# Half-row products for the multipliers, a run of zero products, and finer ranks in a sequence mixer with grouped linear layers

## The chip, the core and the metric

The kernel runs on one NeuronCore of a Trainium2 chip. The metric is the device time of one execution in microseconds (us), lower is better. TensorE (PE) multiplies, VectorE (DVE) and ScalarE (ACT) do arithmetic per element, GpSimd (POOL) does some too, and SyncE (SP) issues nearly all DMA transfers. Everything is float32.

## The reference

```python
x = x + attn(layernorm(x))          # x: 4 x 2048 x 256
x = x + ffn(layernorm(x))
# attn: u, v = split(silu(xn @ uv_w));  out = (u * tno(v)) @ o_w
#   tno: y = irfft(rfft(a, 2n) * rfft(v, 2n))[:n], a long convolution along the sequence;
#   a comes from a small network of the lag (rpe: 4 layers of width 32, layer norm and silu,
#   then @ rpe_out_w), times 0.99**|lag|
# ffn: 8 groups of 1024 tokens; h = (x @ W1[g].T + b1[g]) @ W2[g].T + b2[g]
```

The two linear layers of the ffn have nothing between them, so the kernel multiplies the two matrices of a group into one of 256 x 256. The convolution is done in eight residues r of the sequence: split into rings, a product with cosines and sines (forward), a product with the spectrum of a (the multipliers), a product back, and a recombination.

## The kernel before, in words

`rpe_network` computes the small network for all lags, in two halves of 512 columns: per layer a product `ph`, squares and a copy by ACT (`sq`, `d`), sums `pvar` by PE, an inverse root in eleven small DVE operations (`nve` to `ne`), transposes `pr` and the activation `z`. It is one long dependent chain. `rpe_transform` turns z into the multipliers: DVE forms `rr`, `rq` and `rqd`; per residue r two products make `hp`, DVE multiplies it by phases (`tr`), and products with the weight `wz` make `pa`, which ACT and DVE copy to `am_d` (r = 0) and `am_c` (r = 1 to 7). In `wz`, 128 x 512, the four blocks of 32 rows hold the same weight in one of two halves of the columns, and zeros elsewhere; each `pa` is one product over 128 rows and 512 columns, one for each half k of the frequencies.

`stage_a(b, q)` normalizes a quarter of batch b, transposes it (`pt_a`), and multiplies to `v` (`pv`). `gate` makes u (`pu`, `gt`). `prepare(b, h)` splits v of one half of the channels into rings (DVE). `stage_b(b, h)` gives `forward(r)` (products `pf`, DVE products `y` and `far` with `am`), `backward(r)` (products `acc`), `after(r)` and `end` (DVE: `id`, `iw`, `x0`, `x1`, `x2`, `p`, `tk`; POOL multiplies `gt` by `tk`). `stage_d(b, q)` multiplies `gt` by `ow` (`po`), adds x, normalizes, transposes (`pt_d`), multiplies by the combined matrix `wt` (`pff`), and stores. `stage_w(g)` makes `wt`: four pairs of loads of 256 KB each, a bias by ACT, four products `pw` for each pair. Two pairs fit at once (`WB = 2`); the tables `mats` of the forward and backward products have three buffers each.

No engine's order is that of the program text. Every operation is recorded with a rank, `issue_order` simulates the engines with estimated costs and buffers, and whenever an engine could start several operations it takes the earliest, and of those with the same time the one of lowest rank. The result is a fixed order for each engine, executed in that order; DMA loads stand in SP's order in the same way. Ranks come from `PLACE` by way of `place`: one number for a stage, a quarter or a residue, moved by 20 for each batch. All operations of, say, `forward(r)` (its load, its products, its DVE work) share one.

All recorded operations carry one line number in the profile, L1019, so they are told apart by the names of their tiles.

Of the kernel before, what the change touches and what calls it, by code (L numbers as in the profile page):

```python
# [38 lines left out]
P = 128  # L39
# [10 lines left out]
LAG = 2  # L50
# [56 lines left out]
class Operation:  # L107
# [8 lines left out]
    def cost(self, method):  # L116

        n, psum = columns(self.outs[0]), [a.space == PSUM for a in self.ins]
        if self.dma:
            return (400 if self.engine == "SP" else 460), n * P * 4 / 250  # L120
        if self.engine == "PE":
            return (2 if method == "matmul" else 1) * max(n * 0.84, 110), 165
# [18 lines left out]
class Pool:  # L141
# [5 lines left out]
    def tile(self, shape, dtype, name, **kw):  # L147
# [5 lines left out]

PLACE = {
    "a first": (-99.0, -98.0, -97.0, -96.0),
    "a": (1.74, -2.67, 2.51, 4.46),
    "b": (
        (6.26, 12.16, 4.1, 8.11, 8.37, 13.79, 12.58, 14.11),
        (10.46, 20.27, 15.97, 19.01, 18.94, 18.98, 20.74, 20.97),
    ),  # L160
    "d": (
        (25.35, 27.7),
        (26.25, 28.74),
        (30.44, 33.54),
        (29.38, 31.46),
    ),
    "d last": (
        (42.27, 25.3),
        (65.21, 140.66),
        (46.22, 27.3),  # L170
        (61.26, 28.3),
    ),
    "e": (
        (14.31, 18.21, 18.05, 16.77, 63.85, 71.2, 77.59, 18.72, 12.6, 21.84, 13.2),
        (20.2, 20.5, 20.8, 19.37, 21.4, 39.89, 22.0, 22.54, 22.6, 28.52, 26.75),
    ),
    "e last": (20.2, 100.83, 20.8, 21.1, 21.4, 111.26, 22.0, 22.3, 22.6, 22.9, 23.2),
    "f": (
        (2.08, 2.91, 1.13, 2.05, 4.0, 3.57, 6.5, 6.26),
        (4.04, 18.16, 13.91, 14.02, 14.8, 14.19, 17.79, 18.04),  # L180
    ),
    "g first": (
        (-95.0, 1.77, -95.0, -40.12),
        (-95.0, -95.0, -95.0, -95.0),
    ),
    "g": (
        (6.27, 12.71, 15.72, 5.68),
        (13.81, 10.75, 16.06, 24.4),
    ),
    "p first": (21.76, -4.4, -4.1, -3.8, -3.5, -23.28, -84.19, -2.6, -2.3, -2.0, -1.7, -1.4, -1.1, -0.8, -0.5, 5.66),  # L190
    "p": (
        (55.79, 1.74, 22.08, 23.91, 1.63, 19.64, 38.78, 19.76, 4.06, 16.19, 4.2, 33.43, 39.59, 10.38, 4.51, 33.61),
        (14.03, 5.6, 11.32, 67.54, 11.67, 6.8, 14.31, 16.92, 15.07, 18.9, 70.61, 20.64, 18.53, 20.4, 45.22, 86.73),
    ),
    "rpe": -100.0,
    "rpet": -10.0,
    "w": (-52.41, -95.4, 43.06, 31.0, 55.36, 77.26, 90.91, 188.4),
# [3 lines left out]
def place(stage, *i):  # L201
    if stage in ("rpe", "rpet"):
        return (PLACE[stage],)
    if stage == "w":
        return (PLACE["w"][i[0]] + 0.1 * i[1],) if i[0] < WT else (PLACE["w"][i[0]] + i[1],)
    b, *i = i
    if b == 0 and (stage in ("a", "g") or (stage == "p" and i[0] == 0)):
        stage, i = stage + " first", i[1:] if stage == "p" else i
    elif b == B - 1 and (stage == "d" or (stage == "e" and i[0] == 1)):
        stage, i = stage + " last", i[1:] if stage == "e" else i  # L210
    at = PLACE[stage]
    for n in i:
        at = at[min(n, len(at) - 1)]
    return (20 * b + at,)


# [3 lines left out]
def issue_order(ops, tags):  # L220
# [43 lines left out]
    while len(order) < len(ops):  # L264
# [5 lines left out]
        free[o.engine] = at + o.busy  # L270
        end = at + o.busy + o.tail
# [24 lines left out]
def kernel(  # L296
# [49 lines left out]
    am_c = [const.tile([P, 2, 2, 2, P], F32, name=f"am{r}") for r in range(NR)]  # L346

# [147 lines left out]
    def stage_a(b, q):  # L495
        xnt = xnts[b, q] = tok.tile([P, 2, 4 * P], F32, tag="xnt", bufs=4, name=f"xnt_{b}_{q}")
        xt = early.pop((b, q), None) or load_x(b, q, "xa")
        name = f"a{b}_{q}"
        transposed(normalized(xt, *statistics(xt, name, on_scalar=b > 0), name), xnt, name)
# [11 lines left out]
        r, j0 = divmod(2 * q, 4)  # L511
        for h in range(2):
            lo, hi = (v[:, :, i, h * P : (h + 1) * P] for i in range(2))
            c = cts[b, h]
            G.tensor_tensor(c[:, r, j0 : j0 + 2, 0, :], hi, lo, ALU.add)
            a_, b_ = (lo, hi) if r else (hi, lo)
            G.tensor_tensor(c[:, 1 - r, j0 : j0 + 2, 1, :], a_, b_, ALU.subtract)
# [22 lines left out]
    def rpe_network():  # L540
# [7 lines left out]
        early.update({(0, q): load_x(0, q, "xa") for q in range(2)})  # L548
        decay = t4("decay", "f4")[:, :NT]
        S.dma_start(decay, decays)  # L550

# [17 lines left out]
        for i in range(L + 1):  # L569
            sqs, ds = [], []  # L570
# [25 lines left out]

        z = t4("z", "i4").rearrange("p (j f) -> p j f", f=F)
# [10 lines left out]
    def load_phases():  # L608
        phs = [io.tile([P, 4, D], F32, tag="xd", name=f"ph_{i}") for i in range(2)]
        for i in range(2):  # L610
            for k in range(2):
                S.dma_start(
                    phs[i][k * 64 : (k + 1) * 64], phases[k, 4 * i : 4 * i + 4].partition_broadcast(64)
                )
        return phs

    def rpe_transform(z, phs):
        wz = t4("wz", "i4")[:, : 4 * P].rearrange("p (r c) -> p r c", r=2)
        V.memset(wz, 0.0)
        for s_ in range(4):  # L620
            A.dma_start(wz[s_ * F : (s_ + 1) * F, s_ % 2, :], out_w)
# [41 lines left out]
        for pos, (r, eng) in enumerate(((0, V), (1, V), (1, None), (0, V))):  # L663
            for xx in range(2):
                dst = rq[:, 1:, xx, pos, :]
                if eng is None:
                    A.mul(dst, rv[:, :, r, xx, :], -1.0)
                else:
                    eng.tensor_copy(dst, rv[:, :, r, xx, :])
# [6 lines left out]
        V.tensor_copy(rqd[:, :, 1, 1, :], rdv[:, :, 1, :])  # L676
        A.mul(rqd[:, :, 1, 2, :], rdv[:, :, 1, :], -1.0)


        for r in range(NR + 1):  # L680
            m = ring_mats(r, 0, f"rpe_{r}")
            ph = ps_f.tile([P, 2 * P], F32, tag="pf", name=f"hp{r}")
# [14 lines left out]
            V.tensor_tensor(tr, ph, phs[r // 4][:, r % 4, :], ALU.mult)  # L697
            for k in range(2):
                pa = ps_mm.tile([P, 2, D], F32, tag="mm", name=f"pa{r}_{k}")
                T.matmul(  # L700
                    pa.rearrange("p r c -> p (r c)"),
                    tr[:, k * P : (k + 1) * P],
                    wz.rearrange("p r c -> p (r c)"),
                    start=True,
                    stop=True,
                )
                src = pa.rearrange("p r (h c) -> p h r c", h=2)
                if r == 0:
                    A.copy(am_d[:, :, 0:3:2, k, :], src)
                    V.tensor_copy(am_d[:, :, 1, k, :], src[:, :, 0, :])  # L710
                elif k:
                    A.copy(am_c[r - 1][:, :, :, k, :], src)
                else:
                    V.tensor_copy(am_c[r - 1][:, :, :, k, :], src)
# [7 lines left out]
    def stage_w(g):  # L722
        na, oc = INTER // P, 2
        yield
# [4 lines left out]
        S.dma_start(row, b2[g : g + 1, :].partition_broadcast(P))  # L729
        d = small.tile([P, na], F32, tag="d", bufs=2, name=f"dw_{g}")  # L730
# [4 lines left out]
        for o in range(0, na, oc):  # L735
            w1s = io.tile([P, oc, D], F32, tag="w1", bufs=WB, name=f"w1_{g}_{o}")
            S.dma_start(w1s, w1[g].rearrange("(p a) h -> p a h", a=na)[:, o : o + oc, :])
            w2s = io.tile([P, oc, D], F32, tag="w2", bufs=WB, name=f"w2_{g}_{o}")
            S.dma_start(w2s, w2t[g].rearrange("(p a) h -> p a h", a=na)[:, o : o + oc, :])
            for a in range(oc):  # L740
# [11 lines left out]
            yield  # L752
# [38 lines left out]
    def stage_b(b, h):  # L791
# [10 lines left out]
        def forward(r):  # L802
            m = ring_mats(r, 0, f"{nm}_{r}")
            pf = ps_f.tile([P, 2, 2, P], F32, tag="pf", name=f"pf_{nm}_{r}")
            for k in range(2):
                cols = slice(k * P, (k + 1) * P)
                for xx in range(2):
                    if r == 0:
                        T.matmul(pf[:, k, xx, :], m[:, xx, cols], rs[r][:, k, xx, :], start=True, stop=True)
                    else:  # L810
                        T.matmul(pf[:, k], m[:, xx, cols], rs[r][:, :, xx, :], start=(xx == 0), stop=(xx == 1))
            y = ys[r] = t2(f"y_{nm}_{r}", "y").rearrange("p (k r c) -> p k r c", k=2, r=2)
# [13 lines left out]
        def backward(r):  # L826
            m, y = ring_mats(r, 1, f"{nm}_{r}"), ys.pop(r)
            acc = accs[r] = ps_i.tile([P, 2, 2, P], F32, tag="acc", name=f"acc_{nm}_{r}")
# [14 lines left out]
        def after(r):  # L843
            acc = accs.pop(r)
# [82 lines left out]
    def stage_d(b, q):  # L927
        wt, last = wts[2 * b + q // 2], b == B - 1
        xt = load_x(b, q, "xa" if last and q >= 2 else "xd")
        for j in range(2):  # L930
# [12 lines left out]
        name = f"d{b}_{q}"  # L943
        xns = normalized(xt, *statistics(xt, name, on_scalar=not last), name)
        yield
        transposed(xns, xn2, name, shift=True)
        for j in range(2):
# [8 lines left out]
            if last:  # L956
                S.dma_start(out[b, q][:, r, :], xt[:, r, :])
        if not last:
            S.dma_start(out[b, q], xt)
        yield  # L960
# [3 lines left out]
    def pieces(stage, *rank):  # L964

        n = 0
        while True:
            ops.at(*place(*rank, n))
# [5 lines left out]
    def at(*rank):  # L974
        ops.at(*place(*rank))
# [3 lines left out]
    for q in range(NQ):  # L979
        at("a", 0, q)  # L980
        stage_a(0, q)
    for g in range(WT):
        list(pieces(stage_w(g), "w", g))
# [3 lines left out]
    list(pieces(prepare(0, 0), "p", 0, 0))  # L987
    for b in range(B):
        for h in range(2):
            for q in range(NQ):  # L990
                at("g", b, h, q)
                gate(b, h, [q])
        for h in range(2):
            forward, backward, after, end = stage_b(b, h)
            for r in range(NR + 1 + LAG):
                if r <= NR:
                    at("f", b, h, r)
# [124 lines left out]
```

## Time and profile before

| what | value |
|---|---|
| median of three executions | 589.51 us (589.31 to 590.65) |
| profiled execution, its own time | 589.18 us |
| its span, first to last instruction | 587.3 us |
| PE busy | 563.2 us, 96% |
| DVE busy | 504.4 us, 86% |
| ACT busy | 312.8 us, 53% |
| POOL busy | 149.7 us, 25% |
| DMA, mean | 139 GB/s |

The page gives one profiled execution. A product of float32 stands in it as two records, each with a record of a weight load. A record's duration holds its way through the array too, so the rate of PE is read from the starts of a row of records and not from their durations. Where a busy share is 100%, PE may still run below its rate.

### The profile page before, as it was taken

How to read it: one execution, taken by the hardware profiler on the slowest of the kernel's cores; microseconds unless marked ns; L12 is line 12 of the kernel's file. 1: busy time of each engine (PE TensorE's matmuls, PEld its weight loads, DVE VectorE, ACT ScalarE, POOL GpSimd, SP SyncE). 2: the span in 40 equal slices, each digit the busy share in tenths (PEclk: the TensorE clock that was granted, in tenths of full speed). 3: DMA queues.
4: the chain of work that ended last, by engine and by line, in shares of the span. 5: the costliest groups of instructions: out<-in, count | busy, mean ns of one | idle time of the engine just before them, and what ended most of it. 6: DMA issues, size and time to landing. Idle time of an engine off the chain costs nothing.

```text
span 587.3 us, 8243 instructions
## 1 busy us (share of the span) xinstructions
PE 563.2 (96%) x2620; PEld 457.3 (78%) x2620; DVE 504.4 (86%) x1118; ACT 312.8 (53%) x822; POOL 149.7 (25%) x184
## 2 busy tenths in 40 slices
PE   6899999999997999999999999999999999998797
PEld 3788565887885888787878888778888888787686
DVE  3575984999998799999986999998979999999862
ACT  2779862164322754996545728886348365112162
POOL 0154210011362211123475200106271100020420
PEclk9999999999999999999999999999999999999999
DMA  8731374555454445363541453455443543424202
GB/s 266 204 113 61 89 230 154 157 165 161 142 146 136 109 145 171 108 228 114 157 119 46 153 179 127 145 179 145 125 108 90 193 158 143 149 67 138 78 37 108
DMA packets 39987, 81.36 MB, mean 139 GB/s; under 512 B 5636, under 2 KB 7172, under 8 KB 39944
## 3 DMA queue, kind: packets, MB, share of 16 engines
q1 hardware_dynamic: 39208, 79.91, 44.2%
q10 hardware_dynamic: 736, 0.92, 0.5%
q8 instruction: 21, 0.34, 0.2%
q14 instruction: 22, 0.18, 0.1%
HBM read 72.43 MB, written 8.39 MB: 138 GB/s over the span
## 4 chain that ended last, share of the span: by engine, by line
PE 88%; DMA 7%; ACT 2%; DVE 1%; issue 1%; SPq 0%; ACTq 0%; DVEq 0%
PE acc L1019 18%; PE pf L1019 18%; PE pff L1019 9%; PE pv L1019 9%; PE po L1019 9%; PE pw L1019 7%; PE pu L1019 7%; DMA w<-in_L_ffn_W_dram 6%; PE pt_a L1019 2%; PE pa L1019 2%; PE pt_d L1019 2%; PE ph L1019 2%; PE pvar L1019 1%; PE hp L1019 1%; PE pr L1019 1%; DMA lag_t<-in_lag_rows_dram 1%
## 5 line engine op out<-in xcount | busy, mean ns | idle before, releaser
L1019 PE MATMUL acc<-mats,y 128*128 128x256 f32 (+1 forms) x512 | 114.7, 367 | 0.0
L1019 PEld LDWEIGHTS acc<-mats,y 128*128 128x128 f32 x512 | 91.7, 190 | 14.0 <-issue 2.1
L1019 PE MATMUL pw<-w,w 128*128 128x256 f32 x256 | 65.9, 388 | 11.5 <-DMA w<-in_L_ffn_W_dram 9.7
L1019 POOL TENSOR_TENSOR gt<-gt,tk 128x512 f32<-128x512 f32 x32 | 44.8, 1411 | 122.8 <-DVE tk L1019 122.8
L1019 POOL TENSOR_TENSOR c<-v 128x256 f32<-128x256 f32 x64 | 55.5, 894 | 56.2 <-ACT v L1019 45.8
L1019 PEld LDWEIGHTS pw<-w,w 128*128 128x128 f32 x256 | 46.8, 194 | 21.9 <-ACT w L1019 13.6
L1019 PE MATMUL pv<-uvw,xnt 128*128 128x256 f32 x256 | 60.7, 382 | 0.0
L1019 PE MATMUL po<-ow,gt 128*128 128x256 f32 x256 | 60.2, 379 | 0.0
L1019 ACT ACTIVATE w<-w,dw 128x256 f32<-128x256 f32 x64 | 29.6, 502 | 56.9 <-DMA w<-in_L_ffn_W_dram 56.9
L1019 PE MATMUL pu<-xnt,uvw 128*128 128x512 f32 x128 | 59.8, 592 | 0.0
L1019 PE MATMUL pf<-ra,mats 128*128 128x256 f32 x256 | 58.9, 380 | 0.0
L1019 PE MATMUL pff<-wt,xn 128*128 128x256 f32 x256 | 58.0, 380 | 0.3 <-ACT xn L1019 0.3
L1019 PEld LDWEIGHTS pv<-uvw,xnt 128*128 128x128 f32 x256 | 47.4, 190 | 8.3 <-ACT xnt L1019 1.2
L1019 PEld LDWEIGHTS pf<-ra,mats 128*128 128x128 f32 x256 | 48.2, 190 | 7.0 <-issue 0.5
L1019 PEld LDWEIGHTS pff<-wt,xn 128*128 128x128 f32 x256 | 48.1, 190 | 6.8 <-ACT xn L1019 0.6
L1019 PEld LDWEIGHTS po<-ow,gt 128*128 128x128 f32 x256 | 47.8, 190 | 7.0 <-issue 1.0
L1019 DVE TENSOR_TENSOR y<-y,far 128x256 f32<-128x256 f32 x128 | 51.8, 445 | 0.2
L1019 POOL TENSOR_TENSOR rs_a<-ve_a,mhalf 128x4 f32<-128x4 f32 x16 | 19.8, 1236 | 113.3 <-ACT ve_a L1019 105.2
L1019 POOL TENSOR_TENSOR rs_d<-ve_d,mhalf 128x4 f32<-128x4 f32 x16 | 16.6, 1037 | 115.4 <-ACT ve_d L1019 99.2
L1019 DVE TENSOR_TENSOR y<-pf,am 128x512 f32<-128x512 f32 x56 | 38.3, 684 | 6.5 <-PE pf L1019 5.0
L1019 ACT COPY e<-acc 128x512 f32<-128x512 f32 x24 | 14.0, 584 | 50.5 <-PE acc L1019 43.6
L1019 DVE TENSOR_TENSOR far<-pf,am 128x512 f32<-128x512 f32 x56 | 38.1, 681 | 0.2
(151 smaller groups left out, 1022.0 us busy)
## 6 DMA issues: line engine op xcount, KB each, us to landing
mats<-in_mats_dram SPq DMA_DIRECT2D x128, 256.0 KB, 2.7
w<-in_L_ffn_W_dram SPq DMA_DIRECT2D x64, 256.0 KB, 4.2
xa<-in_x_dram SPq DMA_DIRECT2D x18, 512.0 KB, 3.7
xd<-in_x_dram SPq DMA_DIRECT2D x14, 512.0 KB, 3.5
out_dram<-xd SPq DMA_DIRECT2D x12, 512.0 KB, 2.7
mats_rpe<-in_mats_dram SPq DMA_DIRECT2D x8, 256.0 KB, 4.1
row<-in_L_ffn_b_dram SPq DMA_DIRECT2D x8, 128.0 KB, 4.8
ph<-in_phases_dram SPq DMA_DIRECT2D x4, 256.0 KB, 5.5
```

The lines of the kernel that those rows point to most:

```text
L1019: ops[k].call(*ops[k].args, **ops[k].kw)
```

## The change

1. `wz` becomes 128 x 256: all four blocks of 32 rows hold the weight, with no zeros. The order of the four blocks in `rq` and `rqd` changes, so that rows 0 to 63 of `tr` give the real parts and rows 64 to 127 the imaginary parts. Each residue has four products of 64 rows and 256 columns in place of two of 128 rows and 512 columns. They name a position in the array: rows from 0 or rows from 64. The copies from `pa` are divided by real and imaginary part. The phases are loaded in eight transfers of 128 KB, not in four of 256 KB.
2. Eight products of zeros, 128 x 256, are ranked ahead of everything else.
3. Load, statistics, transposes, products and DVE work of a stage each get a rank of their own, with own values for the first and the last batch, and all are new. In the planner, the cost of a product is halved where it names a position and doubled ahead of 7.5 us, and transfers are taken as 270 bytes per ns of their true number of partitions.

```diff
-            return (400 if self.engine == "SP" else 460), n * P * 4 / 250
+            return (400 if self.engine == "SP" else 460), n * self.outs[0].shape[0] * 4 / 270
...
-            return (2 if method == "matmul" else 1) * max(n * 0.84, 110), 165
+            tiles = 2 if "tile_position" in self.kw else 1
+            return (2 if method == "matmul" else 1) * max(n * 0.84, 110) / tiles, 165
...
-    "rpe": -100.0,
-    "rpet": -10.0,
-    "w": (-52.41, -95.4, 43.06, 31.0, 55.36, 77.26, 90.91, 188.4),
+    "rpe": -91,
+    "rpe.0": -182,
...
+    "w.1": -95.3, "w.1.l.1": -84, "w.1.l.2": -95.1, "w.1.l.3": -58, "w.1.m.1": -95.2, "w.1.m.2": -77, "w.1.m.3": -86,
...
+    "warm": -199,
...
+COLD, WARM_UP = 7500, 8
...
-        free[o.engine] = at + o.busy
-        end = at + o.busy + o.tail
+        busy = o.busy * (2 if o.engine == "PE" and at < COLD else 1)
+        free[o.engine] = at + busy
+        end = at + busy + o.tail
...
-            for k in range(2):
+            for k in range(4):
                 S.dma_start(
-                    phs[i][k * 64 : (k + 1) * 64], phases[k, 4 * i : 4 * i + 4].partition_broadcast(64)
+                    phs[i][k * F : (k + 1) * F], phases[k % 2, 4 * i : 4 * i + 4].partition_broadcast(F)
...
-        wz = t4("wz", "i4")[:, : 4 * P].rearrange("p (r c) -> p r c", r=2)
-        V.memset(wz, 0.0)
+        wz = t4("wz", "i4")[:, :D]
         for s_ in range(4):
-            A.dma_start(wz[s_ * F : (s_ + 1) * F, s_ % 2, :], out_w)
+            A.dma_start(wz[s_ * F : (s_ + 1) * F], out_w)
...
+            pas = [ps_mm.tile([P, 2, D], F32, tag="mm", name=f"pa{r}_{c}") for c in range(2)]
             for k in range(2):
-                pa = ps_mm.tile([P, 2, D], F32, tag="mm", name=f"pa{r}_{k}")
-                T.matmul(
-                    pa.rearrange("p r c -> p (r c)"),
-                    tr[:, k * P : (k + 1) * P],
-                    wz.rearrange("p r c -> p (r c)"),
-                    start=True,
-                    stop=True,
-                )
-                src = pa.rearrange("p r (h c) -> p h r c", h=2)
...
+                for c, pa in enumerate(pas):
+                    rows = slice(c * 2 * F, (c + 1) * 2 * F)
+                    T.matmul(
+                        pa[:, k, :], tr[rows, k * P : (k + 1) * P], wz[rows], start=True, stop=True, tile_position=(c * 2 * F, 0)
+                    )
+            re, im = (pa.rearrange("p k (h c) -> p h k c", h=2) for pa in pas)
+            if r == 0:
+                A.copy(am_d[:, :, 0], re)
+                V.tensor_copy(am_d[:, :, 1], re)
+                A.copy(am_d[:, :, 2], im)
+            else:
+                A.copy(am_c[r - 1][:, :, 1], im)
+                V.tensor_copy(am_c[r - 1][:, :, 0], re)
...
+    at("warm")
+    zeros = const.tile([P, 2 * P], F32, name="zeros")
+    V.memset(zeros, 0.0)
+    warm = ps_w.tile([P, 2, D], F32, tag="w", name="warm")
+    for _ in range(WARM_UP):
+        T.matmul(warm[:, 0, :], zeros[:, :P], zeros, start=True, stop=True)
```

The order of instructions that follows differs on every engine. Some of it: on SP, the loads of `par` and `lag_t`, first and second before, stand fifth and seventh, behind the bias, the row and the first pair of weights of group 1, and the second quarter of x that is loaded is the fourth (`xa_0_3`). On PE, three `pw` of group 1 stand between the zeros and the first `ph`. The first `hp` is that of residue 2, then 4 and 1, with 0 and 5 among the first `pf`. In the last batch the four weight groups of `pw_6` and `pw_7` each stand one place earlier.

## The prediction

> **What bounds the kernel now.** I read the page first: the shares, the slices, the chain.
>
> ```profile
> span 587.3 us, 8243 instructions
> ...
> PE 563.2 (96%) x2620; PEld 457.3 (78%) x2620; DVE 504.4 (86%) x1118; ACT 312.8 (53%) x822; POOL 149.7 (25%) x184
> ...
> PEclk9999999999999999999999999999999999999999
> ...
> PE 88%; DMA 7%; ACT 2%; DVE 1%; issue 1%; SPq 0%; ACTq 0%; DVEq 0%
> ```
>
> PE bounds it, with DVE close behind. Only two things can shorten it: less PE work, or less time in which PE stands or runs slowly. So I counted PE's work. In unbroken stretches of the timeline a record of 256 columns starts every 0.2155 us, one of 512 every 0.43, a transpose or a 4-column record every 0.108. All records at these rates make 549 us; 38.5 us of the span are lost. Where? PE's timeline at the start:
>
> ```profile
> 5.27 3.75 PE L1019 MATMUL ph<-lag_t,w 4*128 4x512 f32 x4 [5.27 <-DMA lag_t<-in_lag_rows_dram]
> 8.94 3.58 PE L1019 MATMUL pvar<-par,sq 128*128 128x4 f32 x16
> 12.85 2.04 PE L1019 MATMUL pw<-w,w 128*128 128x256 f32 x4 [0.33 <-DMA w<-in_L_ffn_W_dram]
> 17.19 1.94 PE L1019 MATMUL pr<-ident,ne 128*128 128x128 f32 x8 [2.30 <-DVE ne L1019]
> ...
> 21.88 1.88 PE L1019 MATMUL ph<-z,bd 128*128 128x512 f32 x4
> ...
> 24.02 1.84 PE L1019 MATMUL pvar<-par,sq 128*128 128x4 f32 x16
> ```
>
> The same four `ph` records take 3.75 us at first and 1.88 at 21.88; sixteen `pvar` take 3.58 and then 1.84. PE runs at half rate until about 21, while the granted clock reads 9 in every slice: the clock row hides it, pairs of equal rows show it. By 21.88 PE has done 6.85 us of full-rate work (`ph` 1.72, `pvar` 1.72, four `pw` products 1.72, `pr` and `pt_a` 0.86 each): 15.0 us of the 38.5 are lost there. The rest, from windows (their length, busy time and records of PE, PEld, DVE, ACT and POOL, then clock, DMA share and GB/s) and the end of the timeline:
>
> ```profile
> 180.00:200.00 20.00, 15.86 (x67) 12.15 (x66) 14.55 (x29) 7.89 (x24) 6.09 (x8) 1.00 0.51 139
> 540.00:550.00 10.00, 5.46 (x23) 4.28 (x24) 9.89 (x15) 2.72 (x6) 3.81 (x3) 1.00 0.55 163
> ```
> ```profile
> 546.19 6.16 POOL L1019 TENSOR_TENSOR gt<-gt,tk 128x512 f32<-128x512 f32 x4 [14.90 <-DVE tk L1019]
> 548.47 1.97 PE L1019 MATMUL pw<-w,w 128*128 128x256 f32 x8 [2.12 <-DMA w<-in_L_ffn_W_dram]
> 550.27 2.75 PE L1019 MATMUL po<-ow,gt 128*128 128x256 f32 x12
> ```
>
> PE loses 4.8 us at 181 to 191 and 5.7 at 537 to 548. The named releaser is the load of weights, but DVE is 9.89 of 10 busy in the second: it is making the `tk` that POOL needs for `gt`, and two `gt` end at about 549.3, so `po` could have begun only 1 us sooner. At the first, two `gt` end at 191.34 and `po` starts at 192.34. Both weight waits are mostly cover. About 4 us follow the last product; the remaining 9 are small gaps.
>
> **The change, part by part.** The sum runs against the profiled execution, 589.18 us, 0.33 below the median of 589.51.
>
> *Multipliers.* The row of `pa`:
>
> ```profile
> L1019 PE MATMUL pa<-wz,tr 128*128 128x512 f32 x32 | 14.5, 592 | 0.0
> ```
>
> 32 records at 0.43 make 13.8 us, with PE full around them. The new form has 64 records of 256 columns: again 13.8 one by one, 6.9 if every pair overlaps. [...] No row shows a drain; the nearest is the tail of a record, 0.380 lasting less 0.2155 spacing, 0.165 us. Nine blocks have 18 changes: 0 to 3.0 us; I take half, 1.5. Net gain 2.8 (full pairs 6.9, no pairing and all drains -3.0). The copies stay one each for ACT and DVE (0.58 and 0.69), DVE loses a memset of `wz` (0.49), two copies of 0.42 become one. Four more phase transfers cost SP 4 x 0.59 us, at a time when it waits for PE's buffers, and they land long before the first `hp`. All this costs nothing while those waits last, at worst 2 us of SP.
>
> *Zeros and the new start.* The memset (0.27, DVE idle until 3.58) lets PE begin near 1.2. Sixteen records take 6.9 us at half rate. [...]
>
> The price is a later chain. On SP `lag_t` is now seventh and needs a free completion slot:
>
> ```profile
> SPq L1019 <- DMA uvw<-in_L_attn_uv_w_dram: 1.5, 1, 1.5
> ```
>
> Before, the ninth transfer (`row`) waited so until 5.10; now the ninth is `lag_t`. Issued then, landing 3 to 4 us later, it is there at 8 to 9, not 5.1. Also, three `pw` stand ahead of `ph` in PE's queue, and with them wait `ph`, ACT's `sq`, DVE's `nve`. Their weights with all ahead and beside them (1.42 MB at some 0.39 MB per us from 2.5) land at 6.1, two ACT biases of 0.5 end at 7.1, three `pw` at 8.5. `ph` then ends at 10.4 and `pvar`, paced by ACT, at 12.1; `nve` also stands behind `nb_a`, whose x lands near 8.5, plus statistics 2.4 and POOL's power 1.0: 12.5. Before, `nve` started at 12.56. The chain is even, and ACT, now full with `xn_a`, gives the second `ph` at about 21.5. By then PE has done five `pw`, six `pv`, `ph`, `pvar`, `pt_a`, `pr`: 9.9 us. Gain 9.9 - 6.85 = 3.0 (0 to 5).
>
> It lasts if PE stays full to the first `hp`. Ahead of that the changed order has 54.1 us of PE work (two `pw_0` groups, 3.45 us, moved behind): 21.5 + 44.2 = 65.8. DVE finished `rq` at 67.9 before. PE work between the third `pvar` and its `pr` falls from 5.9 to 3.5 us, which makes the chain about 2.4 sooner, 65.5. I charge 0.5 for what is late next. The weight wait of 1.3 us at 75.75 stays: two buffers, same distance.
>
> *Ranks after the multipliers.* DVE was 4.46 of 10 busy at 90 to 100, so it can follow. At 181 `pw_2_6` moves behind `po`; the wait for `gt` remains: +0.8. In the last batch the fourth group of `pw_7` moves from after `po` into the time in which `gt` is awaited: 1.7 us less after `po`, but `wt_7` now stands ahead of the last `tk` on DVE: -0.3. Together +1.4. Elsewhere I compared, for each table and weight load, the PE work between its buffer's release and its first product: no table has less than its 2.7 us to landing, and at 180 two short distances fall to one. I give +0.5 (-4 to +5), the largest unknown.
>
> Sum: 3.0 - 0.5 + 2.8 + 0.8 + 1.4 + 0.5 = 8.0. 589.18 - 8.0 = 581.2; with the 0.33, 581.5. I say 581.
>
> **Rivals.**
> *No pairing.* The records run one after another and drain: -3.0 for +2.8, 587. For: no trace shows pairs. [...] Chance 0.10.
> *The zeros don't open the clock,* or it falls shut while PE waits for x: start 0, 584.5. [...] Chance 0.12.
> *The order fits better than I can see,* body and boundaries give 5 more: 574 to 577. Chance 0.13. Beyond 571 DVE forbids it: some 12 us idle from z to the first `po` of batch 0.
> *Slower: draining is dear.* Each of the 18 changes would cost a full stop with a refill instead of a tail. The other parts give 9.5 with pairing, so from 0.53 us each it decides; at 0.7 it is 12.6, so 592.6. [...] Against: nothing in the trace is near it. With fixed orders that wait on each other in the re-ranked body as the same sign's lesser cause, chance 0.13.
>
> **How the numbers follow.** The forecast has 0.52 (577.5 to 585). Faster by over 0.3%, below 587.7, about what a measurement can tell from no change: 0.52 + 0.12 + 0.13 and half of no pairing: 0.82. Same 0.06, slower 0.12. The range leaves out most of the slower case and the last of the better one: 571.5 to 588.
>
> **What would show it.** Right: sixteen zero records, the later half spaced 0.2155; first full `ph` about 1.9 us and not 3.75; second `ph` near 21.5; first `hp` near 66; `pa` records that overlap, all within about 10 us of PE; `po` of the last batch about 6 us sooner than 550. Wrong: `pvar` still 3.58, gaps of over 0.3 us around each `pa` block, `hp` waiting for DVE, new waits of PE for `mats`, or `nve` after 14.

## The result: slower by 0.8%

| | before | changed |
|---|---|---|
| median, 11 executions each | 589.31 us (588.22 to 590.65) | 594.18 us (590.44 to 595.9) |
| ratio | | 1.0081 (95%: 1.0060 to 1.0102) |
| profiled execution, its own time | 589.18 us | 595.61 us |
| its span | 587.3 us | 593.8 us |

I forecast 581. The sum was 8.0 us of gain against the profiled execution, and that execution became 6.4 longer. The page of the changed kernel, the same rows as before:

```profile
span 593.8 us, 8318 instructions
...
PE 571.7 (96%) x2668; PEld 462.4 (78%) x2668; DVE 503.1 (85%) x1117; ACT 313.2 (53%) x822; POOL 153.2 (26%) x184
...
PEclk8699999999999999999999999999999999999999
...
PE 83%; DMA 8%; DVE 4%; ACT 3%; issue 1%; SPq 0%; ACTq 0%; DVEq 0%
```

PE is busier by 8.5 us, of which zeros at full rate explain only 3.45, and the clock row, which was 9 throughout, shows 8 and 6 in its first two slices (14.8 us each). DVE and ACT, 1% and 2% of the chain before, now hold 4% and 3%. PE's timeline at the start says what happened there; a line gives start, length, operation, count, and in brackets the idle time ahead of it with what ended it:

```profile
1.19 6.70 PE L1110 MATMUL warm<-zeros 128*128 128x256 f32 x16 [1.19 <-DVE zeros L1110]
10.36 2.60 PE L1110 MATMUL pw<-w,w 128*128 128x256 f32 x6 [2.47 <-DMA w<-in_L_ffn_W_dram]
12.88 3.78 PE L1110 MATMUL ph<-lag_t,w 4*128 4x512 f32 x4
16.59 1.87 PE L1110 MATMUL pvar<-par,sq 128*128 128x4 f32 x8
...
28.18 1.13 PE L1110 MATMUL ph<-z,bd 128*128 128x512 f32 x2 [0.51 <-ACT z L1110]
```

The zeros end at 7.89; I had taken 6.3 to 8.0. Then PE stands for 2.47 us, and the first `ph` starts at 12.88, not at 8.5, and takes 3.78, where four `ph` records of the kernel before took 3.75 at half rate and 1.88 at full rate. The second `ph` starts at 28.18; I had said 21.5. The windows of the same stretch (busy time of PE, PEld, DVE, ACT and POOL, then granted clock, DMA share and GB/s) show the clock:

```profile
8.00:10.00 2.00, 0.00 (x0) 0.00 (x0) 0.00 (x0) 1.78 (x3) 0.00 (x0) 1.00 0.87 281
10.00:12.00 2.00, 1.65 (x5) 1.38 (x6) 1.42 (x7) 0.41 (x2) 0.00 (x0) 0.67 1.02 406
12.00:14.00 2.00, 2.00 (x5) 0.83 (x4) 1.97 (x11) 0.00 (x0) 0.00 (x0) 0.50 0.94 301
22.00:24.00 2.00, 2.00 (x10) 1.78 (x9) 1.79 (x9) 1.03 (x3) 1.06 (x3) 0.50 0.64 191
24.00:26.00 2.00, 2.00 (x13) 1.69 (x12) 1.24 (x3) 2.00 (x5) 0.00 (x0) 0.92 0.93 273
```

By the trace's own record of the clock, the closed time (a granted clock of 0.5) is 13.65 us, from 10.7 to 24.3. What PE waited for stands on the other engines, DVE first, then ACT:

```profile
10.48 0.29 DVE L1110 TENSOR_REDUCE rmean<-par 128x4 f32<-128x128 f32 x1 [8.53 <-DMA par<-in_rpe_par_dram]
21.05 0.19 DVE L1110 TENSOR_SCALAR nve<-pvar 128x32 f32<-128x32 f32 x1 [5.08 <-PE pvar L1110]
```
```profile
8.21 1.28 ACT L1110 ACT_TABLE_LOAD   x1 [8.21 <-DMA w<-in_L_ffn_W_dram]
9.50 0.91 ACT L1110 ACTIVATE w<-w,dw 128x256 f32<-128x256 f32 x2
```

`par` lands at 10.4; before, DVE had it at 3.58. It is issued at 2.6, fifth on SP, and takes 7.9 us behind weights and a row of biases; before, issued first, it took 2.8. `nve` starts at 21.05, against 12.56 before.

To see where the rest went I repeated the count of lost time on both timelines, up to the end of the last product: time elapsed less PE's work at full rate. The zeros count as lost, and two records that overlap count as a negative loss. Differences are of unrounded values.

| stretch | before | changed | difference | forecast |
|---|---|---|---|---|
| start to behind the first `hp` | 17.1 | 22.4 | +5.3 | -2.5 |
| multipliers, to 126 us | 0.3 | -0.7 | -1.0 | -2.8 |
| to the end of batch 0's body, 180 us | 1.6 | 3.0 | +1.5 | -0.5 |
| boundary of batch 0, 180 to 195 us | 4.9 | 4.8 | -0.1 | -0.8 |
| to 535 us | 3.3 | 4.0 | +0.7 | in the -0.5 above |
| last batch | 7.3 | 7.3 | 0.0 | -1.4 |
| sum | 34.5 | 40.9 | +6.4 | -8.0 |

The spans differ by 6.5; the other 0.1 follows the last product. The start is over half of the miss, 7.8 of 14.4.

### The profile page after: what moved, and what is told of

It is laid out like the page before. It is cut to its first block, busy times and chain, and to the rows that moved or that the text cites. A ratio compares the mean times of both kernels' runs of the same rounds, so it can differ in the third digit from the quotient of the medians.

```text
span 593.8 us, 8318 instructions
## 1 busy us (share of the span) xinstructions
PE 571.7 (96%) x2668; PEld 462.4 (78%) x2668; DVE 503.1 (85%) x1117; ACT 313.2 (53%) x822; POOL 153.2 (26%) x184
## 4 chain that ended last, share of the span: by engine, by line
PE 83%; DMA 8%; DVE 4%; ACT 3%; issue 1%; SPq 0%; ACTq 0%; DVEq 0%
PE pf L1110 16%; PE acc L1110 16%; PE pff L1110 9%; PE pu L1110 8%; PE po L1110 8%; PE pw L1110 8%; PE pv L1110 7%; DMA w<-in_L_ffn_W_dram 7%; PE pt_d L1110 2%; PE pt_a L1110 2%; PE ph L1110 2%; PE pa L1110 2%; PE pvar L1110 1%; PE hp L1110 1%; DMA mats<-in_mats_dram 1%
## 5 line engine op out<-in xcount | busy, mean ns | idle before, releaser
L1110 PE MATMUL acc<-mats,y 128*128 128x256 f32 (+1 forms) x512 | 116.2, 367 | 2.0 <-DMA mats<-in_mats_dram 1.4
L1110 PE MATMUL pw<-w,w 128*128 128x256 f32 x256 | 68.5, 401 | 11.6 <-DMA w<-in_L_ffn_W_dram 9.9
L1110 PEld LDWEIGHTS pw<-w,w 128*128 128x128 f32 x256 | 48.4, 199 | 23.7 <-ACT w L1110 12.7
L1110 PE MATMUL pv<-uvw,xnt 128*128 128x256 f32 x256 | 62.4, 384 | 0.0
L1110 PE MATMUL pf<-ra,mats 128*128 128x256 f32 x256 | 61.0, 380 | 0.0
L1110 PE MATMUL pff<-wt,xn 128*128 128x256 f32 x256 | 60.1, 381 | 0.3 <-ACT xn L1110 0.3
L1110 POOL TENSOR_TENSOR rs_d<-ve_d,mhalf 128x4 f32<-128x4 f32 x16 | 18.8, 1175 | 115.6 <-ACT ve_d L1110 98.0
L1110 PEld LDWEIGHTS pu<-xnt,uvw 128*128 128x128 f32 x128 | 24.1, 190 | 17.7 <-issue 16.3
```

The costliest lines, as they stand in the source:

```text
L1110: ops[k].call(*ops[k].args, **ops[k].kw)
```

## Experiments

The runs on the changed kernel leave its order of instructions as it is but for the edit shown, which is made on the planned list, behind the planner. In the three runs on the kernel before with half rows, the planner runs on the new products, and the order within the multipliers changes too. The code shown is the main lines of each edit, and the comments in it are added here. Each run has its ratio to the kernel before, run on the same chip. The medians of that kernel differ by up to 3.5 us between chips, so ratios are compared, and traces of two chips only stretch by stretch.

| run | median us | kernel before | ratio (95%) |
|---|---|---|---|
| no_zeros | 597.23 | 592.47 | 1.0085 (1.0056 to 1.0114) |
| zeros_14 | 593.05 | 592.47 | 1.0001 (0.9982 to 1.0020) |
| rpe_early | 592.60 | 592.47 | 1.0004 (0.9985 to 1.0023) |
| before_half_rows | 589.69 | 592.47 | 0.9953 (0.9930 to 0.9976) |
| late_zeros | 596.32 | 591.53 | 1.0064 (1.0040 to 1.0088) |
| table_early | 594.25 | 591.53 | 1.0050 (1.0030 to 1.0070) |
| start_rebuilt | 590.67 | 591.53 | 0.9984 (0.9969 to 0.9999) |
| half_rows_and_zeros | 586.44 | 591.53 | 0.9922 (0.9896 to 0.9948) |
| loads_unblocked | 587.10 | 589.01 | 0.9970 (0.9959 to 0.9981) |
| unblocked_and_zeros | 586.90 | 589.01 | 0.9961 (0.9950 to 0.9973) |
| half_rows_denser | 586.84 | 589.01 | 0.9958 (0.9942 to 0.9973) |
| changed_again | 593.88 | 589.01 | 1.0076 (1.0061 to 1.0092) |

**no_zeros: are the zeros worth anything?**

```diff
+            if ops[k].outs[0].tensor.name.startswith("warm"):
+                continue
             ops[k].call(*ops[k].args, **ops[k].kw)
```

> The changed kernel with the eight zero products left out, every other instruction in the same order. Theory A (late loads: the start is lost because par, lag_t and x come after the weights, so ph starts 7.6 us later than before): the zeros only fill a time in which PE would have idled, the first pw again near 10.4, the second ph again near 28 (28.2 with zeros), time within 2 us of the changed kernel, about 594. Theory B (clock: the zeros open it at 7.3 and the stop behind them lets it fall at 10.7, so it is the stop that costs): nothing has opened it, so the same; if instead the zeros still help later, the second ph comes 1 to 3 us later and the time is 596 to 597.

1.0085 without them, 1.0081 with them; the second `ph` at 27.98 instead of 28.18. Eight zero products ahead of a stop of 2.47 us are worth nothing that these ratios, each good to 0.2 or 0.3%, can tell.

**zeros_14: the stop filled.**

```diff
+        extra = 6
         for k in issue_order(ops, tags):
+            if ops[k].outs[0].tensor.name.startswith("warm"):
+                for _ in range(extra):
+                    ops[k].call(*ops[k].args, **ops[k].kw)
+                extra = 0
```

> The changed kernel with 14 zero products instead of 8, the rest in the same order: 13.5 records at half rate to 7.3, the others at 0.2155 to about 10.3, when the first weights are ready, so that PE never stops. Theory A (late loads): pw, ph and pvar run at full rate, but ph still waits for par until about 11.7, nve still stands behind the statistics of x; second ph 2 to 3 us sooner, time 591 to 592. Theory B (the fallen clock is the main loss): the 13.5 us at half rate from 10.7 to 24.2 vanish, 6 to 7 us of PE; time 587 to 588. Should the clock fall all the same in ph and pvar, which fill few rows or columns, there is no gain.

```profile
1.18 4.81 PE L1113 MATMUL warm<-zeros 128*128 128x256 f32 x12 [1.18 <-DVE zeros L1115]
5.83 3.62 PE L1115 MATMUL warm<-zeros 128*128 128x256 f32 x16
10.33 1.56 PE L1115 MATMUL pw<-w,w 128*128 128x256 f32 x6 [0.88 <-ACT w L1115]
11.82 1.98 PE L1115 MATMUL ph<-lag_t,w 4*128 4x512 f32 x4
...
24.26 1.02 PE L1115 MATMUL ph<-z,bd 128*128 128x512 f32 x2
```

`pw` starts when it did, but takes 1.56 for 2.60, and `ph` 1.98 for 3.78: the clock is open. It falls later, from 15.4 to 22.2, for 6.83 us and not 13.65. `nve` starts at 16.67, the second `ph` at 24.26, 3.9 sooner; 3.3 of that still stand at 120 us, 2.4 at 200, 1.1 at the end of the profiled execution. Against the changed kernel's 1.0081 the median gains 0.8%, about 4.7 us; against no_zeros, on the same chip, 4.2. So six more products that compute nothing take back the whole loss, though half of the closed time is still there: what they remove of it is worth 4 to 5 us, less than theory B's 6 to 7 for all of it, more than theory A's 2 to 3.

**rpe_early: the chain ahead of the weights.**

```diff
-        for k in issue_order(ops, tags):
...
+        ahead = ("par_", "lag_t", "rmean", "w0", "bd", "ph0_", "sq0_", "d0_", "pvar0")
+        moved = [k for k in order if k <= pvar and name(k).startswith(ahead)]
...
+        front = zeros + first + moved
+        for k in front + [k for k in order if k not in set(front)]:
```

> The changed kernel with the loads of par and lag_t first on SP, and ph, sq, d and pvar of the first layer ahead of pw and of the bias of the weights on PE and ACT; all else in the changed order, the zeros too. Theory A (late loads): ph near 7.9 right behind the zeros, nve near 16 (behind the statistics of x) instead of 21.05, second ph near 23 instead of 28.2, time about 589. Theory B (clock): PE stops between pvar and pw and the clock falls again; second ph near 26, time 592. Theory C (the new ranks behind the start lose it): start sooner, but the time stays at 593 to 594.

```profile
6.88 1.98 PE L1118 MATMUL ph<-lag_t,w 4*128 4x512 f32 x4
...
23.36 1.12 PE L1118 MATMUL ph<-z,bd 128*128 128x512 f32 x2 [0.74 <-ACT z L1118]
```

`ph` is at full rate right behind the zeros; `nve` is at 15.71, the ratio 1.0004. As theory A said, to 0.4 us for `nve` and the second `ph`, and `ph` came 1.0 sooner still. But the clock was open longer here too (in the start it falls once, 15.6 to 19.0), so this run and the last one share a part of their gain. Behind the start it fell three more times, for 3.41 us each, and of the 4.8 us at the second `ph` 1.8 are left at the end.

**table_early: the table load that stands behind ACT's wait.**

```diff
+            if ops[k].outs[0].tensor.name.startswith("mhalf"):
+                nc.scalar.activation(early_table, mhalf, AF.Square)
```

> The changed kernel with one small activation on ACT at its start, so that the table load of 1.28 us stands ahead of the first wait for weights and not behind it. Theory A (late loads): pw starts near 9.1 instead of 10.4, but par lands at 10.4 and ph can't start before 11.6; gain about 1 us. Theory B (clock): PE stops for 1.2 us instead of 2.5 behind the zeros; if the clock therefore stays open, ph and pvar take half the time, and the gain is 4 us as with 14 zeros (ratio near 1.001); if not, 1 us (1.007).

ACT, then PE:

```profile
1.25 1.28 ACT L1113 ACT_TABLE_LOAD   x1 [1.25 <-PEq L1200]
8.39 0.91 ACT L1111 ACTIVATE w<-w,dw 128x256 f32<-128x256 f32 x2 [5.64 <-DMA w<-in_L_ffn_W_dram]
```
```profile
10.22 2.34 PE L1111 MATMUL pw<-w,w 128*128 128x256 f32 x6 [2.27 <-DMA w<-in_L_ffn_W_dram]
```

A miss for both. The bias is done at 9.30, and `pw` still starts at 10.22: it waits for the second of its two loads. The stop is 2.27 instead of 2.47, the clock falls, the second `ph` comes at 27.80. The ratio, 1.0050, is lower than the trace explains (0.4 us); its interval overlaps that of the changed kernel, and I don't read a gain from it. Its 22 executions show something else, the price of the clock with no edit at all: the four with a mean granted clock of 0.980 to 0.982 span 594.8 to 596.4 us, the five of 0.994 to 0.997 span 589.0 to 591.3.

**start_rebuilt: x early as well.**

```diff
+        x0 = [k for k in order if name(k).startswith("xa_0_0") and ops[k].dma]
+        front = zero + first + moved + x0
...
+        late = [next(k for k in order if ops[k].engine == e and reads(k, "w1_1_2")) for e in ("ACT", "PE")]
...
+        spot = max(n for n, k in enumerate(order) if name(k).startswith("pt_a0_0_2")) + 1
+        order[spot:spot] = late
```

> The changed kernel with par, lag_t and the first quarter of x first on SP, the first rpe layer ahead of pw on PE and ACT, and the fifth pw with its bias moved behind the first transposes; zeros first, all else as changed. Theory A (late loads): x is there at 7.1 and not 12.3, nve at 12.5 to 13, second ph near 20 to 21 instead of 28.2; 6 to 7 us less than the changed kernel at the first hp, of which what the later waits for loads leave is 5: ratio 0.998 to 1.000. Theory C (the new ranks behind the start lose it): not below 1.000 whatever the start.

PE's rows, then DVE's:

```profile
6.96 1.98 PE L1125 MATMUL ph<-lag_t,w 4*128 4x512 f32 x4
8.86 1.95 PE L1125 MATMUL pvar<-par,sq 128*128 128x4 f32 x16
...
21.66 1.02 PE L1125 MATMUL ph<-z,bd 128*128 128x512 f32 x2
```
```profile
7.51 0.75 DVE L1125 BATCH_NORM_STATS2 st_a<-xa 128x6 f32<-128x256 f32 x2 [1.91 <-DMA xa<-in_x_dram]
13.50 0.17 DVE L1125 TENSOR_SCALAR nve<-pvar 128x32 f32<-128x32 f32 x1
```

x is there at 7.5 instead of 12.3, the second `ph` at 21.66, which is where I had put it in the changed kernel. PE is 5.9 to 6.2 us ahead of the changed kernel at the multipliers and 4.5 at the end; the ratio is 0.9984 instead of 1.0081. The clock falls for 3.41 us in this start, from 15.8 to 19.2, and once more at 186.4. The order of loads and of the first layer, with what it does to the clock, is the largest single cause; how much of it is the clock alone these runs do not separate.

**before_half_rows: part 1 alone, on the kernel before.**

```diff
+                for c, pa in enumerate(pas):
+                    rows = slice(c * 2 * F, (c + 1) * 2 * F)
+                    T.matmul(
+                        pa[:, k, :], tr[rows, k * P : (k + 1) * P], wz[rows], start=True, stop=True, tile_position=(c * 2 * F, 0)
+                    )
```

> The kernel before with part 1 of the change alone: pa in half rows, four products of a residue in the order of the two halves in turn; ranks and start as before, no zeros. By the trace of the changed kernel a block of four takes 1.08 us in place of 1.72, without a drain: eight blocks save up to 5.1, less one that is broken, 4.5; some of it is lost where DVE and ACT can't make tr and the copies faster. Expected 585 to 586. If changing the place in the array cost a drain each time, or DVE were the bound here, 588 to 590.

The kernel before, then this run:

```profile
75.75 1.97 PE L1019 MATMUL pw<-w,w 128*128 128x256 f32 x8 [1.29 <-DMA w<-in_L_ffn_W_dram]
...
80.13 1.89 PE L1019 MATMUL pw<-w,w 128*128 128x256 f32 x8
81.86 1.88 PE L1019 MATMUL pa<-wz,tr 128*128 128x512 f32 x4
```
```profile
79.88 1.99 PE L1022 MATMUL pw<-w,w 128*128 128x256 f32 x8
81.80 1.13 PE L1022 MATMUL pa<-wz,tr 64*128 64x256 f32 x8
82.87 1.99 PE L1022 MATMUL hp<-mats_rpe,rq 128*128 128x256 f32 x8
84.70 0.59 PE L1022 MATMUL pw<-w,w 128*128 128x256 f32 x2
...
87.18 1.13 PE L1022 MATMUL pa<-wz,tr 64*128 64x256 f32 x6 [0.40 <-DVE am L1022]
```

Start to start, the eight records take 1.07 us, near the 1.08 expected; five records in a row, at 0.2155 each, would make the same. The block is not that, though. In the trace the single records start at 81.80, 81.81, 82.12, 82.13, 82.34, 82.35, 82.56 and 82.56: four pairs, in which every record overlaps another. The rest is lost where PE changes between products of 128 rows and of 64. The eight `pw` ahead of the block take 1.92 us start to start (79.88 to 81.80), where eight took 1.73 before; the eight `hp` behind it take 1.83. Counted on the single records, the last one ahead of a change costs 0.09 more than its 0.2155 and the first one behind it 0.105 more, at all 12 changes of this run. A change thus costs 0.195 us, and "without a drain" was a wrong reading: a change has a price, and on what it goes no run shows.

The ratio 0.9953 is 2.8 us, with an interval from 1.4 to 4.1. On PE, the stretch from the first `hp` to the first `pf` is 2.2 us shorter, 23.9 for 26.1. Of this 1.3 is the wait for weights at 75.75, which the new order no longer has. The other 0.9 is what the half rows leave: 24 pairs gain 5.2, twelve changes cost 2.3, three waits for the copies `am` (0.35 to 0.40) cost 1.1, and smaller waits the rest. With the products shorter, DVE is the slower one there.

**late_zeros: the clock falls a second time.** In the changed kernel the wait at batch 0's boundary has moved into one piece, and this is what follows it:

```profile
186.81 1.88 PE L1110 MATMUL pu<-xnt,uvw 128*128 128x512 f32 x4
191.58 5.38 PE L1110 MATMUL pw<-w,w 128*128 128x256 f32 x16 [2.88 <-DMA w<-in_L_ffn_W_dram]
196.79 1.46 PE L1110 MATMUL po<-ow,gt 128*128 128x256 f32 x6
```

Sixteen records take 5.2 us instead of 3.45; the clock is closed for 3.41 us from 191.6. Before, the same wait came as three of 1.3 to 1.5, of which this is the first, and the granted clock stayed at 1.00:

```profile
184.43 1.97 PE L1019 MATMUL pw<-w,w 128*128 128x256 f32 x8 [1.53 <-DMA w<-in_L_ffn_W_dram]
```

```diff
+        fill = {"w1_2_2": 7}                     # w1_2_2: read by the second group of pw_2
...
+                for _ in range(fill.pop(key)):
+                    nc.tensor.matmul(ops[k].args[0], zeros[:, :P], zeros, start=False, stop=False)
```

> The changed kernel with seven zero products added into the sum of pw_2 (they add nothing to it) ahead of its second group, in the time from 188.7 to 191.6 in which PE waits for weights and after which the granted clock falls to half for 3.4 us. Clock theory: the clock stays at 1.00 there, the 16 records of pw take 3.45 in place of 5.38, all behind them comes 1.7 us sooner; time 1 to 1.7 us less than the changed kernel's (ratio to before near 1.006). If the clock falls by another cause, or po waits for gt anyway, nothing changes (1.0085).

```profile
189.14 3.19 PE L1113 MATMUL pw<-zeros 128*128 128x256 f32 x14
192.16 3.62 PE L1114 MATMUL pw<-w,w 128*128 128x256 f32 x16
195.61 1.67 PE L1114 MATMUL po<-ow,gt 128*128 128x256 f32 x7
```

The zeros add nothing to the sum of `pw_2`. `pw` takes 3.45 and `po` comes 1.8 us sooner relative to what precedes it, as expected; the clock does not fall. Of the total, 1.0064 against 1.0081 and 1.0076, the interval does not tell it from nothing.

**half_rows_and_zeros: the two sound parts on the old order.**

```diff
+        for _ in range(8):
+            nc.tensor.matmul(warm[:, 0, :], zeros[:, :P], zeros, start=True, stop=True)
+        fill = [("w1_1_0", 4), ("pr0_0", 3)]     # 4 more ahead of pw; 3 into pw_1, ahead of pr
```

> The kernel before with half-row pa, and zeros where PE stands in its start: eight products ahead of the first ph (1.2 to about 6.9), four between pvar and pw, three between pw and pr. If the clock opens at 5.3 to 7.3 and stays open, ph 1.9 and pvar 1.9 instead of 3.75 and 3.58, nve near 10.8 instead of 12.6, second ph near 19 instead of 21.9; gain 2 to 3 us on the half rows alone, ratio 0.990 to 0.992. If the clock falls in ph and pvar, ph only starts 1.5 us later: 0.997.

```profile
7.22 1.98 PE L1037 MATMUL ph<-lag_t,w 4*128 4x512 f32 x4
9.13 3.31 PE L1037 MATMUL pvar<-par,sq 128*128 128x4 f32 x16
12.29 3.76 PE L1034 MATMUL warm<-zeros 128*128 128x256 f32 x8
```

`ph` at full rate, but the clock falls from 9.4 to 16.3; `nve` at 12.47 comes only 0.3 sooner than in before_half_rows. The second `ph` comes at 21.06, 1.5 sooner, and PE is 1.5 to 1.8 us ahead from there to the end. It beats both kernels.

**half_rows_denser.**

```diff
+        fill = [("sq0_0", 2), ("w1_1_0", 4), ("pr0_0", 4)]     # 2 between ph and pvar; 4, not 3, ahead of pr
```

> The kernel before with half rows and zeros as in half_rows_and_zeros, with two more products between ph and pvar and one more ahead of pr. There the clock fell from 9.4 to 16.3, because ph and pvar fill few rows or columns. If every 3.4 us hold 1.5 us of full products now, it stays open: pvar 1.9 instead of 3.3, second ph near 19.5 instead of 21.1; ratio 0.990 against 0.9922. If it falls all the same, 0.993.

The clock stays open through the start: `pvar` 1.84 instead of 3.31. But then PE waits 0.97 for ACT's `z`, and the second `ph` comes at 20.79, only 0.3 sooner: the chain is ACT's. The median is 586.84 beside 586.44 of the run before it, each with its own runs of the kernel before; I can't tell the two apart. In the profiled execution of the denser one the clock fell in the waits of the last batch, from 539.1 to 542.5 and from 545.9 to 552.8, and PE fell about 4 us behind the other run there.

**loads_unblocked and unblocked_and_zeros: is what is left in the new order?** Both are built on start_rebuilt.

```diff
+        sp = [k for k in order if ops[k].engine == "SP" and name(k).startswith(("mats0_1_0_2", "mats1_0_0_1"))]
...
+        for a, b in (sp, (bias, copy)):          # a goes behind b; bias: of w1_2_0, copy: e6_0_1
+            order.remove(a)
+            order.insert(order.index(b) + 1, a)
```

> The changed kernel with the rebuilt start, and two moves by one place behind it: on SP the table mats1_0_0_1, for which PE waits 1.42 us at 126, goes ahead of mats0_1_0_2, a table of the next batch that stands before it and waits for its own buffer; on ACT the copy e6_0_1, for which PE waits 1.57 us at 173.9, goes ahead of a bias that waits for weights. If the new ranks lose by such neighbours (theory C in its remaining part), 1.4 and 1.0 us come back there, together 2: ratio 0.995 against 0.9984. If loads are late by the amount of data that stands before them, x above all, the first move gives nothing and the second up to 1: 0.997.

> The same with seven zero products added into pw_2 in the wait for weights near 182 to 186, behind which the clock fell for 3.41 us. The clock theory: it stays open, 1.7 us less from there, of which the last batch takes back up to 0.7: ratio 0.992 to 0.993. Without an effect: as the run before it.

start_rebuilt, at the two places, and then loads_unblocked:

```profile
126.45 1.75 PE L1125 MATMUL acc<-mats,y 128*128 128x256 f32 x7 [1.42 <-DMA mats<-in_mats_dram]
...
173.95 1.99 PE L1125 MATMUL acc<-mats,y 128*128 128x256 f32 x8 [1.57 <-ACT e L1125]
```
```profile
126.95 1.97 PE L1132 MATMUL acc<-mats,y 128*128 128x256 f32 x8 [1.16 <-DMA mats<-in_mats_dram]
...
173.21 1.99 PE L1132 MATMUL acc<-mats,y 128*128 128x256 f32 x8
```

The first move is a miss: the table still lands late, with 1 MB of weights and x issued ahead of it. The second takes its wait away; PE gains 1.7 us between 150 and 174. In the profiled execution of loads_unblocked the clock did not fall at the boundary, at a stop of 2.69 us, where in start_rebuilt it had fallen at one of 2.65. There unblocked_and_zeros had nothing to win; 0.9961 beside 0.9970 is no difference.

**changed_again**, for comparison on the last chip.

> The changed kernel as it is, measured beside the others on this chip. By its runs so far: ratio 1.008, clock closed from 10.6 to 24.4 and from 191.5 to 195.0.

1.0076; closed from 10.9 to 24.6 and from 191.8 to 195.2, within 0.3 us of the first trace.

## Why the prediction was wrong, step by step

- **The price of a later chain** is the step that failed. It has three terms. The loads: I let 1.42 MB run at 0.39 MB per us and had the weights at 6.1. The first landed at 8.1 and the second at 10.2; from 2 to 10 us the transfers made 238, 286, 161 (from 6 to 8) and 281 GB/s for the windows of 2 us, a mean of 0.24 MB per us. The rate I took was the best window of the old start (397 GB/s from 4 to 6); the windows beside it made 293 and 330. Why it is not kept stays open: in rpe_early, where `par` no longer stands behind the weights, the windows from 4 to 8 make 261 and 128. `par`: I followed `lag_t`, whose issue at 4.97 came as forecast, and left out `par`, without which there is no `w0` and no `ph`; it landed at 10.4. And x: I had 8.5, it came at 12.3. I said "the chain is even" at 12.5; `nve` was at 21.05. Of these 8.5 us rpe_early takes back 5.3 (`nve` at 15.71) and start_rebuilt 7.6 (13.50).
- **The clock.** The 3.0 us of the start rest on zeros that end between 6.3 and 8.0 and on full rate for all that follows. No run shows that term; it was my assumption, and the kernel before spoke against it: 7.25 us of `ph` and `pvar`, from 5.27 on, ran at half rate, and so did what followed, until 21.4. What the runs show: the zeros start every 0.427 us up to 7.3 and every 0.2155 behind it, and end at 7.89. With a stop of 2.47 us behind them the granted clock is 0.50 from 10.7 to 24.3; with one of 0.88, in zeros_14, it is 0.50 from 15.4 to 22.2. The rival said as much as "or it falls shut while PE waits for x", at 0.12. It fell while PE waited for weights, and the rival's price (start 0, 584.5) was far too small, since I had priced it without the late loads. I had asked when the clock opens and not when it closes. Nor was PE idle all the time ahead of the fall: the last 3.41 us ahead of it, from 7.26 to 10.67, held 0.7 us of products.
- **Multipliers.** The 2.8 that before_half_rows gave is the 2.8 of the sum, and that is luck: the sum has it as a gain of 4.3 from products that partly overlap, less 1.5 for the changes, and no run shows that overlap. In the traces all records of a full block pair, and the 26 pairs of the changed kernel gain 5.6 us. The changes were taken too cheap: each of the 18, from products of 128 rows to a block of 64 or back, costs 0.195 us, 3.5 in all, though far from the 0.53 at which the rival of a dear drain begins. Small waits take 1.4 more, so that the stretch comes out at -0.7, 1.0 better than before and not 2.8. On the old order, 1.3 of the gain was a wait for weights that went away with the order.
- **Boundary of batch 0** (+0.8): a gain of 0.1. Moving work from ahead of the wait to behind it joined three waits into one, and the clock fell on it. late_zeros shows the 1.8 us.
- **Last batch** (+1.4): from the first full `po` to the end it is 1.5 us shorter, 35.5 for 37.0, as I said. But the waits ahead of `po` are as long as before, 5.6 for 5.7:

```profile
546.08 1.97 PE L1110 MATMUL pw<-w,w 128*128 128x256 f32 x8 [0.19 <-DMA w<-in_L_ffn_W_dram]
549.70 1.97 PE L1110 MATMUL pw<-w,w 128*128 128x256 f32 x8 [1.66 <-DMA w<-in_L_ffn_W_dram]
553.47 1.97 PE L1110 MATMUL pw<-w,w 128*128 128x256 f32 x8 [1.81 <-DMA w<-in_L_ffn_W_dram]
556.50 1.97 PE L1110 MATMUL pw<-w,w 128*128 128x256 f32 x8 [1.06 <-ACT w L1110]
558.30 4.02 PE L1110 MATMUL po<-ow,gt 128*128 128x256 f32 x17
```

  The group that left the end did not fill a wait; another took its place in it, and each still waits for its pair of loads.
- **Other ranks** (a gain of 0.5, from -4 to +5): a loss of 2.1. I had looked at loads against buffers. One cost is ACT's order, a copy that PE needs behind a bias that waits for weights: 0.68 us in the changed kernel, 1.57 in start_rebuilt, where PE comes earlier, and none in loads_unblocked. The rest of it stays open, as does why half rows with the old ranks (0.9953) do at least as well as start_rebuilt with one wait removed (0.9970).

Start 7.8, boundary 0.7, last batch 1.4, ranks 2.6 and multipliers 1.8 make 14.4 by the unrounded values, which is -8.0 to +6.4.

## What to carry over

Filling PE ahead of its first real product paid only with a short stop behind it: with one of 2.47 us eight zero products gave nothing (1.0081 with them, 1.0085 without), and with one of 0.88 fourteen took back 0.8%. So find what the first product needs, all of its operands, and when each lands, at a rate measured over the whole stretch (0.24 MB per us here) and not in its best window (0.39). When work is moved around a wait, ask whether several short stops become one long one (here 1.53, 1.32 and 1.29 us became 2.88). When a length agrees with a forecast, look at the single records too: five records in a row, and four pairs with a change of rows at either end, both come to about 1.07 us. And when a queue is re-ranked, look on each in-order engine for what the next engine needs, standing behind something that waits for a load.

## What I had not expected of the hardware

- The granted clock was 0.50 for 3.41, 6.83 or 13.65 us at a time, one, two or four times 3.41, and the length of a stop alone did not decide. Stops of 2.47 us at 7.9, 2.65 in start_rebuilt and 2.88 at 188.7 came ahead of a closed clock; one of 2.69 in loads_unblocked and stops of 1.1 to 1.8 at the end of the changed kernel did not. Stretches of 3.41 us, laid end to end from a change of the clock, sort these cases: the open times of the changed kernel and of the kernel before, 167.25, 399.36 and 566.61 us, are 49, 117 and 166 of them. Counted over all 14 traces, and without the stretches that hold `ph` and `pvar` of 4 rows or columns, those at whose end the clock closed held at most 1.25 us of products (rpe_early, 548.1 to 551.5), and those at whose end it stayed open at least 1.30 (before_half_rows, 538.7 to 542.2); in the changed kernel it was 0.7 (7.3 to 10.7) and 0.4 (188.2 to 191.6) against at least 1.5 (550.0 to 553.4). The stop of 2.69 lies across an edge at 184.7 and leaves 1.5 us of products in one stretch and 2.4 in the next; that of 2.65 leaves 0.6 in one. This is a count; how the chip decides was not measured.
- The clock closed behind a busy PE too. In half_rows_and_zeros PE was full from 1.2 on, and the clock fell at 9.4, in `ph` (4 rows) and `pvar` (4 columns); in the run with two full products between them it stayed open there. Four stretches of 3.41 us with 2.4 to 3.1 us of work, much of it such thin products, ended with the clock closing; how much these count was not measured.
- The granted clock in the profile reads 1.00 until its first change: it was 1.00 while the zeros started every 0.427 us, up to 7.3, and up to 21.4 in the kernel before, where `ph` took 3.75 us at 5.27 and 1.88 at 21.88.
- Float32 products in two row halves pair record by record, within 0.03 us of each other in 25 of the 26 pairs of the changed kernel. A change between 128 rows and 64 costs 0.195 us, the same at 17 of that kernel's 18 changes (the other stands at a wait) and at the 12 of before_half_rows.
